# A row of attention scores on all partitions: one transpose for four batches and GpSimd partition broadcasts, in place of four transposes

## The chip, the core and the metric

The kernel runs on one core of a Trainium2 chip. The core has five engines that work side by side and wait for one another by semaphores: PE (TensorE, matrix products and transposes, with its weight loads shown as PEld), DVE (VectorE), ACT (ScalarE), POOL (GpSimd) and SP (SyncE, which only issues DMAs here). The metric is the device time of one launch in microseconds. A profile records one execution; its span runs from the first to the last instruction.

## The reference, cut to what matters

The input is x, 128 batches of 128 nodes with 256 features in float32, and adj, a 128 x 128 matrix of 0 and 1 for every batch. There are four layers, each followed by `x = layernorm(x + layer(x, adj))`. The first is a gated graph network: three steps of a product with the adjacency and a GRU cell. The other three are graph attention layers, which differ only in details; one of them is

```python
def _L1_gnn_ref(h, adj, W, a):
    Wh = jnp.einsum('bnf,of->bno', h, W)
    a1, a2 = (a[:Fout], a[Fout:])
    f_i = Wh @ a1
    f_j = Wh @ a2
    e = f_i[:, :, None] + f_j[:, None, :]
    e = jnp.where(e > 0, e, ALPHA * e)
    e = jnp.where(adj == 0, NEG_INF, e)
    attention = jax.nn.softmax(e, axis=2)
    h_prime = jnp.einsum('bij,bjo->bio', attention, Wh)
```

The change concerns the line that makes e. The nodes i lie on the partitions, so f_i is one number per partition. f_j has to stand as a row, the same on every partition. It is at first computed as one number per partition too.

## The kernel before

**Tiling.** Four batches make a group (G = 4), so a group's tensors are 128 partitions by 512 columns (4 x 128 nodes) or by 1024 (4 x 256 features). There are 32 groups. For each, `gru(g)` describes the three recurrent steps and the first layer norm, and `gat(g)` the three attention layers.

**Order.** The loops do not emit instructions. They describe operations to a planner (`Plan`): the engines that can do it with a duration for each in ns, the buffers read and written, and a priority. `Plan.order()` then runs a list schedule with these durations over all 32 groups at once, takes the most urgent ready operation for each engine, hands out buffers from fixed pools (26 of tag `k2`, 18 of `k4`, 3 PSUM banks of tag `bank`, and so on), and the instructions are emitted in that order. On the chip each engine works through its own list in order. So whatever an operation waits for holds up everything behind it on its engine. Three settings shape the order:

- `LATENCY` adds 200 to 250 ns where an operation follows one on another engine. `MARGIN`, 300 ns, is added on top for operations of PE only.
- `own` reserves buffers of each tag for the oldest stage still at work. There is one setting for recurrent stages and one for attention stages.
- `stage(g, n)` gives the priority. It is g for the first 28 groups, so an older group goes first; the last four groups (`LAST = 4`) go step by step together instead.

Operations of POOL, and those of DVE that are marked `port=BOTH`, are never planned at the same time.

**One attention layer of one group**, by lines. L635 multiplies x by a weight vector and sums along the row, eight times (four batches, f_j first and then f_i), into the small tile f with columns [batch, 0 for f_i and 1 for f_j]. In layers 1 and 2, L639 scales f by the reciprocal deviation of the rows, which POOL makes as a power at L389. L648 makes the rows: for each batch a transpose by PE of the column of f_j, repeated 128 times, into a PSUM bank. L653 adds the mask to it, writes e and takes the row maximum (DVE, one per batch). L657 adds f_i and applies the leaky slope (ACT). L666 and L670 make the negative maximum (DVE, 4 columns). L674 takes the exponential with its sum (ACT). L681 transposes e on PE, L686, L690 or the copy of L287/L289 take it out of PSUM, L711 multiplies it by x, L722 by the layer's weights, and L728 adds the residual. L417 to L428 and L389 then give the next deviation. L473 holds the products of the GRU, L478 the sums over them, L443 the sums of block halves that these products need, L526 the products with the adjacency, L607 and L380 further transposes. The two small additions of L401 (layer norm) and L421 (first attention layer) run on POOL.

Of the kernel before, what the change touches and what calls it, by code (L numbers as in the profile page):

```python
# [1 line left out]

# [20 lines left out]

FAR = -5.0 * 2.0 ** 97
EPS = 1e-5
SLOPE = 0.2
# [21 lines left out]
class Plan:  # L48
# [4 lines left out]

    LATENCY = {"PE": 250, "ACT": 220, "DVE": 200, "POOL": 250, "SP": 4000}

    MARGIN = 300

    def __init__(self, slots, own):
        self.free = {t: list(range(n)) for t, n in slots.items()}
# [139 lines left out]
def adj_resnorm_kernel(  # L199
# [14 lines left out]
    nc = tc.nc  # L214
    B = x.shape[0]
    NG = B // G
    LAST = 4
# [48 lines left out]
    wa = here(consts.tile([P, 3, 2, D], F32, name="wa"))  # L266
# [126 lines left out]
    def layernorm(y, dst, prio):  # L393
        mv, ve, shift = Buf("mv", G, 2), Buf("v", G), Buf("v", G)
        for b in range(G):
            st = Buf("st", 6)
            plan.op({"DVE": 330}, lambda e, b=b, st=st: nc.vector.bn_stats(T(st), T(y)[:, b, :]),
                    reads=[(y, b)], writes=[st], prio=prio)
            plan.op({"DVE": 110}, lambda e, b=b, st=st: nc.vector.bn_aggr(T(mv)[:, b, :], T(st)),
                    reads=[st], writes=[(mv, b)], prio=prio)  # L400
        plan.op({"POOL": 229}, lambda e: nc.gpsimd.tensor_scalar(T(ve), T(mv)[:, :, 1], EPS, None, op0=ALU.add),  # L401
                reads=[(mv, b) for b in range(G)], writes=[ve], prio=prio)
        rstd = power(ve, prio)
        plan.op({"DVE": 100}, lambda e: nc.vector.scalar_tensor_tensor(
            T(shift), T(mv)[:, :, 0], -1.0, T(rstd), op0=ALU.mult, op1=ALU.mult),
            reads=[(mv, b) for b in range(G)] + [rstd], writes=[shift], prio=prio)
        for b in range(G):
            plan.op({"ACT": 500}, lambda e, b=b: nc.scalar.activation(  # L408
                T(dst)[:, b, :], T(y)[:, b, :], AF.Identity, bias=T(shift)[:, b:b + 1], scale=T(rstd)[:, b:b + 1]),
                reads=[(y, b), shift, rstd], writes=[(dst, b)], prio=prio)  # L410

    def deviation(y, before, prio):

        ss, ve = Buf("v", G), Buf("v", G)
        for b in range(G):
            jx = Buf("jx", D)
            plan.op({"ACT": 490}, lambda e, b=b, jx=jx: nc.scalar.activation(  # L417
                T(jx), T(y)[:, b, :], AF.Square, accum_out=T(ss)[:, b:b + 1]),
                reads=[(y, b)], writes=[jx, (ss, b)], prio=prio)
        if before is None:  # L420
            plan.op({"POOL": 229}, lambda e: nc.gpsimd.tensor_scalar(  # L421
                T(ve), T(ss), 1.0 / D, EPS, op0=ALU.mult, op1=ALU.add),
                reads=[(ss, b) for b in range(G)], writes=[ve], prio=prio)
        else:
            eps = Buf("v", G)
            plan.op({"DVE": 100}, lambda e: nc.vector.tensor_scalar(T(eps), T(before), EPS, None, op0=ALU.mult),
                    reads=[before], writes=[eps], prio=prio)
            plan.op({"DVE": 100}, lambda e: nc.vector.scalar_tensor_tensor(  # L428
                T(ve), T(ss), 1.0 / D, T(eps), op0=ALU.mult, op1=ALU.add),
                reads=[(ss, b) for b in range(G)] + [eps], writes=[ve], prio=prio)  # L430
        return ve
# [191 lines left out]
    def gat(g, xc, no, stage):  # L623


        ve, rstd = None, None
        for l in range(3):
            prio = stage(g, STEPS + l)
            if g == 0:
                score_weights(l, prio)  # L630
            f = Buf("f", G, 2)
            for h in (1, 0):
                for b in range(G):
                    fx = Buf("fx", D)
                    plan.op({"DVE": 345}, lambda e, b=b, h=h, l=l, f=f, fx=fx, xc=xc: nc.vector.scalar_tensor_tensor(  # L635
                        T(fx), T(xc)[:, b, :], 1.0, T(wa)[:, l, h, :], op0=ALU.mult, op1=ALU.mult,
                        accum_out=T(f)[:, b, h:h + 1]), reads=[(xc, b), (wa, l)], writes=[fx, (f, 2 * b + h)], prio=prio, port=BOTH)
                if l:
                    plan.op({"DVE": 100}, lambda e, h=h, f=f, rstd=rstd: nc.vector.tensor_mul(  # L639
                        T(f)[:, :, h], T(f)[:, :, h], T(rstd)), reads=[(f, 2 * b + h) for b in range(G)] + [rstd],  # L640
                        writes=[(f, 2 * b + h) for b in range(G)], prio=prio)
# [4 lines left out]
            def fn(e, b_=b_, f=f):  # L646
                for b in range(G):
                    nc.tensor.transpose(T(b_)[:, b * P:(b + 1) * P],  # L648
                                        T(f)[:, b, 1:2].to_broadcast([P, P]), ident)
            plan.op({"PE": 440}, fn, reads=[(f, 2 * b + 1) for b in range(G)], writes=[b_], prio=prio)  # L650

            for b in range(G):
                plan.op({"DVE": 215}, lambda e, b_=b_, b=b, e_=e_, top=top: nc.vector.tensor_tensor_reduce(  # L653
                    T(e_)[:, b, :], T(b_)[:, b * P:(b + 1) * P], T(no)[:, b, :], 1.0, 3 * FAR, ALU.add, ALU.max,
                    T(top)[:, b:b + 1]), reads=[b_, no], writes=[(e_, b), (top, b)], prio=prio)
            for b in range(G):
                plan.op({"ACT": 285}, lambda e, b=b, f=f, e_=e_: nc.scalar.activation(  # L657
                    T(e_)[:, b, :], T(e_)[:, b, :], AF.Prelu, bias=T(f)[:, b, 0:1], alpha=SLOPE),
                    reads=[(f, 2 * b), (e_, b)], writes=[(e_, b)], prio=prio)
            if l == 1:  # L660

# [2 lines left out]
                    T(some), T(top), 0.5 * FAR, None, op0=ALU.is_gt),  # L664
                    reads=[(top, b) for b in range(G)], writes=[some], prio=prio)
            plan.op({"DVE": 100}, lambda e, f=f, top=top: nc.vector.scalar_tensor_tensor(  # L666
                T(top), T(top), -1.0, T(f)[:, :, 0], op0=ALU.mult, op1=ALU.subtract),
                reads=[(top, b) for b in range(G)] + [(f, 2 * b) for b in range(G)],
                writes=[(top, b) for b in range(G)], prio=prio)
            plan.op({"DVE": 100}, lambda e, top=top, nmax=nmax: nc.vector.scalar_tensor_tensor(  # L670
                T(nmax), T(top), SLOPE, T(top), op0=ALU.mult, op1=ALU.min),
                reads=[(top, b) for b in range(G)], writes=[nmax], prio=prio)
            for b in range(G):
                plan.op({"ACT": 390}, lambda e, b=b, e_=e_, nmax=nmax, den=den: nc.scalar.activation(  # L674
                    T(e_)[:, b, :], T(e_)[:, b, :], AF.Exp, bias=T(nmax)[:, b:b + 1],
                    accum_out=T(den)[:, b:b + 1]), reads=[(e_, b), nmax], writes=[(e_, b), (den, b)], prio=prio)
            b_ = bank()
# [74 lines left out]

# [41 lines left out]
```

## Time and profile before

| what | us |
|---|---|
| median of 3 runs (2683.05 to 2686.83) | 2685.42 |
| the profiled execution, whole | 2684.54 |
| its span | 2682.8 |
| mean granted TensorE clock | 0.996 of full speed |
| L648, the four transposes: 384 instructions on PE | 58.2 busy |
| L473, the GRU products on PE | 2400.3 busy, two groups of 4032 |
| L653 on DVE: 384 instructions | 89.2 busy |
| POOL in all: 618 instructions | 549.7 busy |

Busy times of PE are sums of durations of matmuls that overlap, as these are pipelined; starts in a timeline show what one of them holds. A line name such as L648 is a line of the kernel file before. In a row of groups the columns are line, engine, operation, output and inputs, shapes and count, then busy us and mean ns, then the idle time of the engine just before, and what ended it.

### The profile page before, as it was taken

Reading aid. Unit: us, or ns where it says so; the run is one execution under the profiler, and the core shown is the slowest. Engines: PE = TensorE matmul, PEld = TensorE weight load, DVE = VectorE, ACT = ScalarE, POOL = GpSimd, SP = SyncE. Lnnn points to the kernel's source line nnn. Section 1 sums busy time; section 2 is a strip of 40 time slices with the busy share of each in tenths; the row PEclk is TensorE's granted clock in tenths of the full one; section 3 lists DMA queues with packets and bytes.
Section 4 is the critical chain, followed back from the end, with each engine's and each line's share of the span. In section 5 each row is a group of like instructions: output and inputs, shape, how many; then the busy total and the mean of one; then the engine's idle time right before and its main releaser. Section 6 shows DMA issues by size and latency. Waiting matters only on the chain.

```text
span 2682.8 us, 41895 instructions
## 1 busy us (share of the span) xinstructions
PE 2650.4 (99%) x14536; PEld 2367.5 (88%) x14536; DVE 2069.0 (77%) x6111; ACT 1611.6 (60%) x4453; POOL 549.7 (20%) x618
## 2 busy tenths in 40 slices
PE   8999999999999999999999999999999999999988
PEld 7888888898898888898889888988988898988877
DVE  5677677887777877778877778777878777786787
ACT  4555666565656666566556566656666665655467
POOL 1122122221122221122211122211222211231111
PEclk9999999999999999999999999999999999999999
DMA  3100000000000000000000001000000000000000
GB/s 110 32 17 20 28 13 28 21 25 28 14 27 21 24 28 21 21 28 21 24 28 21 21 20 28 24 22 19 29 21 25 28 21 17 19 6 24 17 1 32
DMA packets 70102, 65.35 MB, mean 24 GB/s; under 512 B 2689, under 2 KB 68225, under 8 KB 69889
## 3 DMA queue, kind: packets, MB, share of 16 engines
q1 hardware_dynamic: 69456, 62.66, 7.7%
q8 instruction: 114, 1.87, 0.3%
q14 instruction: 100, 0.81, 0.1%
q10 hardware_dynamic: 432, 0.01, 0.0%
HBM read 45.89 MB, written 16.78 MB: 23 GB/s over the span
## 4 chain that ended last, share of the span: by engine, by line
PE 93%; DVE 4%; ACT 1%; issue 1%; DMA 0%; POOL 0%; POOLq 0%; SPq 0%; ACTq 0%; DVEq 0%
PE gate L473 63%; PE bank L722 11%; PE bank L526 6%; PE bank L711 6%; PE bank L607 3%; PE bank L681 1%; PE bank L648 1%; DVE fx L635 1%; PE bank L380 1%; PE bank L338 1%; DVE k L728 1%; DVE k L289 0%; DVE k L568 0%; DVE k L478 0%; DVE k L653 0%
## 5 line engine op out<-in xcount | busy, mean ns | idle before, releaser
L473 PE MATMUL gate<-k,whs 128*128 128x256 f32 x4032 | 1201.1, 380 | 2.4 <-DVE k L478 1.9
L473 PE MATMUL gate<-k,wcs 128*128 128x256 f32 x4032 | 1199.2, 379 | 0.0
L473 PEld LDWEIGHTS gate<-k,wcs 128*128 128x128 f32 x4032 | 766.1, 190 | 104.0
L473 PEld LDWEIGHTS gate<-k,whs 128*128 128x128 f32 x4032 | 730.4, 190 | 84.5 <-DVE k L478 3.1
L478 DVE TENSOR_TENSOR k<-gate,k 128x512 f32<-128x512 f32 x576 | 389.3, 684 | 207.9 <-PE gate L473 184.0
L287 ACT COPY k<-bank 128x512 f32<-128x512 f32 (+1 forms) x401 | 229.5, 584 | 206.8 <-PE bank L607 91.3
L722 PE MATMUL bank<-gwT,k 128*128 128x256 f32 x1536 | 348.8, 380 | 1.0 <-DVE k L289 0.8
L722 PEld LDWEIGHTS bank<-gwT,k 128*128 128x128 f32 x1536 | 290.4, 190 | 42.2 <-DVE k L289 1.8
L552 ACT ACTIVATE k<-k,brz 128x512 f32<-128x512 f32 (+1 forms) x384 | 225.6, 622 | 166.3 <-DVE k L478 164.7
L389 POOL TENSOR_TENSOR v<-v,neghalf 128x4 f32<-128x4 f32 x128 | 134.4, 1050 | 857.7 <-DVE v L428 840.3
L635 DVE SCALAR_TENSOR_TENSOR fx<-k,wa 128x256 f32<-128x256 f32 x768 | 285.9, 426 | 24.3 <-ACT k L408 24.2
L417 ACT ACTIVATE jx<-k 128x256 f32<-128x256 f32 x384 | 156.5, 408 | 231.0 <-DVE k L728 230.7
L534 ACT COPY k<-gate 128x512 f32<-128x512 f32 x288 | 167.6, 582 | 192.8 <-PE gate L473 188.4
L443 POOL TENSOR_TENSOR k<-k,k 128x256 f32<-128x256 f32 x229 | 175.9, 789 | 450.0 <-DVE k L289 223.2
L728 DVE SCALAR_TENSOR_TENSOR k<-bank,v,k 128x256 f32<-128x256 f32 x384 | 167.2, 476 | 106.8 <-PE bank L722 106.6
L289 DVE COPY k<-bank 128x512 f32<-128x512 f32 x219 | 150.1, 686 | 114.0 <-PE bank L711 88.6
L586 POOL TENSOR_TENSOR k<-k,k 128x512 f32<-128x512 f32 x90 | 133.3, 1492 | 303.4 <-ACT k L581 284.2
L711 PEld LDWEIGHTS bank<-k,k 128*128 128x128 f32 x1536 | 187.6, 194 | 7.7 <-DVE k L728 1.9
L711 PE MATMUL bank<-k,k 128*128 128x128 f32 x1536 | 191.2, 278 | 2.2 <-DVE k L728 1.1
L588 DVE SCALAR_TENSOR_TENSOR k<-k,k 128x512 f32<-128x512 f32 x192 | 170.1, 886 | 2.2 <-POOL k L586 1.1
L674 ACT ACTIVATE k<-k,v 128x128 f32<-128x128 f32 x384 | 148.9, 389 | 30.8 <-DVE v L670 30.2
L581 ACT ACTIVATE k<-k,bi 128x512 f32<-128x512 f32 x192 | 138.3, 721 | 47.1 <-DVE k L578 36.9
(86 smaller groups left out, 3012.9 us busy)
## 6 DMA issues: line engine op xcount, KB each, us to landing
xs<-in_x_dram SPq DMA_DIRECT2D x32, 512.0 KB, 3.8
k<-in_x_dram SPq DMA_DIRECT2D x32, 512.0 KB, 3.8
out_dram<-k SPq DMA_DIRECT2D x32, 512.0 KB, 2.9
adj<-in_adj_dram SPq DMA_DIRECT2D x32, 256.0 KB, 2.8
k<-in_gnn_wT_dram SPq DMA_DIRECT2D x3, 256.0 KB, 4.8
k<-in_w_ihT_dram SPq DMA_DIRECT2D x2, 384.0 KB, 5.8
k<-in_w_hhT_dram SPq DMA_DIRECT2D x2, 384.0 KB, 6.0
k<-in_gat_w_dram SPq DMA_DIRECT2D x3, 256.0 KB, 4.6
```

What stands on the lines that cost most here:

```text
L287: nc.scalar.copy(dst, src)
L443: nc.vector if e == "DVE" else nc.gpsimd).tensor_tensor(T(t)[:, j, :], a(), b(), ALU.subtract),
L473: nc.tensor.matmul(T(dst)[:, j * H:(j + 1) * H], T(w)[:, m, gt, :], moving(m, ms)[1](), start=first and n == 0, stop=n == len(todo) - 1, s ...
L478: plan.op({"DVE": 630}, lambda e: nc.vector.tensor_add(T(o)[:, :, j * H:(j + 1) * H], T(b_).rearrange("p (g n) -> p g n", g=2), T(part).re ...
L526: nc.tensor.matmul(T(b_)[:, b * P:(b + 1) * P], src, T(am)[:, b, :], start=True, stop=True)
L534: plan.op({"ACT": 500}, lambda e: nc.scalar.copy(T(dst), T(src)), reads=[src], writes=[(dst, 0), (dst, 1)], prio=prio)
L552: nc.scalar.activation(T(o)[:, gt, n0:n1], src(), AF.Tanh, bias=brz[:, gt * KC + c:gt * KC + c + 1], scale=0.5)
L588: plan.op({"DVE": 620}, lambda e, d=d, o=o: nc.vector.scalar_tensor_tensor(T(d), T(o)[:, 1, :], 1.0, T(d), op0=ALU.add, op1=ALU.mult), rea ...
L635: plan.op({"DVE": 345}, lambda e, b=b, h=h, l=l, f=f, fx=fx, xc=xc: nc.vector.scalar_tensor_tensor(T(fx), T(xc)[:, b, :], 1.0, T(wa)[:, l, ...
L711: nc.tensor.matmul(T(b_)[:, b * P:(b + 1) * P], T(xc)[:, b, c * P:(c + 1) * P], T(pT)[:, b, :], start=True, stop=True)
L722: nc.tensor.matmul(T(b_)[:, (b - b0) * D:(b - b0 + 1) * D], T(aT[k])[:, b * P:(b + 1) * P], T(gwT)[:, l, k, :], start=(k == 0), stop=(k == ...
L728: nc.vector.scalar_tensor_tensor(T(y)[:, b, :], T(b_)[:, (b - b0) * D:(b - b0 + 1) * D], T(rden)[:, b:b + 1], T(xc)[:, b, :], op0=ALU.mult ...
```

## The change

For the first 28 groups, f is 128 columns wide (32 per batch, zero but for two), f_j is now column 0 of a batch's 32 and f_i column 1. One transpose of the whole f puts the f_j of batch b on partition 32 b. ACT or DVE copies this 128 x 128 block from PSUM to a buffer of tag `k2` (`row`), and four `partition_broadcast` on POOL spread one partition each over the 128 partitions of e, where the operation of L653 then reads it and writes it in place. The last four groups keep the four transposes. POOL's broadcast belongs to a library that is loaded once at the start, after the identity matrix has been made; the two additions [...] move from POOL to DVE. The planner's settings change with it: MARGIN, the reserved buffers, and a priority that is 1.5 groups earlier for attention stages.

```diff
-    MARGIN = 300
+    MARGIN = 500
...
-    own = ({"k2": 12, "k4": 5, "gate": 2, "v": 5, "fx": 0, "jx": 0, "st": 0}, {"k2": 4, "k4": 3, "v": 5, "fx": 0, "jx": 0, "st": 0})
-    floats = {"gru": 0, "k4": 1024, "xs": 1024, "fx": 256, "jx": 256, "f": 8, "mv": 8, "st": 6, "v": 4}
+    own = ({"k2": 9, "k4": 4, "gate": 2, "bank": 1, "v": 5, "fx": 0, "jx": 0, "st": 0}, {"k2": 2, "k4": 2, "bank": 1, "v": 5, "fx": 0, "jx": 0, "st": 0})
+    floats = {"gru": 0, "k4": 1024, "xs": 1024, "fx": 256, "jx": 256, "f": 128, "mv": 8, "st": 6, "v": 4}
...
+    for t in slots["f"]:
+        nc.vector.memset(t, 0.0)
...
     ident = consts.tile([P, P], F32)
-    make_identity(nc, ident)
...
-        plan.op({"POOL": 229}, lambda e: nc.gpsimd.tensor_scalar(T(ve), T(mv)[:, :, 1], EPS, None, op0=ALU.add),
+        plan.op({"DVE": 100}, lambda e: nc.vector.tensor_scalar(T(ve), T(mv)[:, :, 1], EPS, None, op0=ALU.add),
...
-            plan.op({"POOL": 229}, lambda e: nc.gpsimd.tensor_scalar(
+            plan.op({"DVE": 100}, lambda e: nc.vector.tensor_scalar(
...
-            f = Buf("f", G, 2)
+            f = Buf("f", G, P // G)
...
-                        accum_out=T(f)[:, b, h:h + 1]), reads=[(xc, b), (wa, l)], writes=[fx, (f, 2 * b + h)], prio=prio, port=BOTH)
+                        accum_out=T(f)[:, b, 1 - h:2 - h]), reads=[(xc, b), (wa, l)], writes=[fx, (f, 2 * b + h)], prio=prio, port=BOTH)
...
+            if g < NG - LAST:
+
+                plan.op({"PE": 115}, lambda e, b_=b_, f=f: nc.tensor.transpose(
+                    T(b_)[:, 0:P], T(f).rearrange("p b h -> p (b h)"), ident),
+                    reads=[(f, 2 * b + 1) for b in range(G)], writes=[b_], prio=prio)
+                row = Buf("k2", P)
+                plan.op({"ACT": 250, "DVE": 200}, lambda e, b_=b_, row=row: copy(e, T(row), T(b_)[:, 0:P]),
+                        reads=[b_], writes=[row], prio=prio)
                 for b in range(G):
-                    nc.tensor.transpose(T(b_)[:, b * P:(b + 1) * P],
-                                        T(f)[:, b, 1:2].to_broadcast([P, P]), ident)
-            plan.op({"PE": 440}, fn, reads=[(f, 2 * b + 1) for b in range(G)], writes=[b_], prio=prio)
+                    plan.op({"POOL": 300}, lambda e, row=row, b=b, e_=e_: nc.gpsimd.partition_broadcast(
+                        T(e_)[:, b, :], T(row)[b * P // G:b * P // G + 1, 0:P]), reads=[row], writes=[(e_, b)], prio=prio)
+                rows, keys, port = (lambda b, e_=e_: T(e_)[:, b, :]), lambda b: [], BOTH
+            else:
+                def fn(e, b_=b_, f=f):
+                    for b in range(G):
+                        nc.tensor.transpose(T(b_)[:, b * P:(b + 1) * P],
+                                            T(f)[:, b, 0:1].to_broadcast([P, P]), ident)
+                plan.op({"PE": 440}, fn, reads=[(f, 2 * b + 1) for b in range(G)], writes=[b_], prio=prio)
+                rows, keys, port = (lambda b, b_=b_: T(b_)[:, b * P:(b + 1) * P]), lambda b, b_=b_: [b_], ("POOL",)
...
-                plan.op({"DVE": 215}, lambda e, b_=b_, b=b, e_=e_, top=top: nc.vector.tensor_tensor_reduce(
-                    T(e_)[:, b, :], T(b_)[:, b * P:(b + 1) * P], T(no)[:, b, :], 1.0, 3 * FAR, ALU.add, ALU.max,
-                    T(top)[:, b:b + 1]), reads=[b_, no], writes=[(e_, b), (top, b)], prio=prio)
+                plan.op({"DVE": 215}, lambda e, rows=rows, b=b, e_=e_, top=top: nc.vector.tensor_tensor_reduce(
+                    T(e_)[:, b, :], rows(b), T(no)[:, b, :], 1.0, 3 * FAR, ALU.add, ALU.max,
+                    T(top)[:, b:b + 1]), reads=keys(b) + [no, (e_, b)], writes=[(e_, b), (top, b)], prio=prio, port=port)
...
-        return g if g < tail else tail + n, 2 * g + (n >= STEPS)
+        return (g + (-1.5 if n >= STEPS else 0) if g < tail else tail + n), 2 * g + (n >= STEPS)
...
+        make_identity(nc, ident)
+
+        nc.gpsimd.load_library(library_config.all_libraries[10])
```

More of the change, by code (lines that the diff above doesn't have):

```diff
@@ L4 @@
 import concourse.tile as tile
+from concourse import library_config
 from concourse import mybir
@@ L636, in gat @@
                         T(fx), T(xc)[:, b, :], 1.0, T(wa)[:, l, h, :], op0=ALU.mult, op1=ALU.mult,
-                        accum_out=T(f)[:, b, h:h + 1]), reads=[(xc, b), (wa, l)], writes=[fx, (f, 2 * b + h)], prio=prio, port=BOTH)
+                        accum_out=T(f)[:, b, 1 - h:2 - h]), reads=[(xc, b), (wa, l)], writes=[fx, (f, 2 * b + h)], prio=prio, port=BOTH)
                 if l:
                     plan.op({"DVE": 100}, lambda e, h=h, f=f, rstd=rstd: nc.vector.tensor_mul(
-                        T(f)[:, :, h], T(f)[:, :, h], T(rstd)), reads=[(f, 2 * b + h) for b in range(G)] + [rstd],
+                        T(f)[:, :, 1 - h], T(f)[:, :, 1 - h], T(rstd)), reads=[(f, 2 * b + h) for b in range(G)] + [rstd],
                         writes=[(f, 2 * b + h) for b in range(G)], prio=prio)
@@ L644, in gat @@
             b_ = bank()
-            def fn(e, b_=b_, f=f):
-                for b in range(G):
-                    nc.tensor.transpose(T(b_)[:, b * P:(b + 1) * P],
-                                        T(f)[:, b, 1:2].to_broadcast([P, P]), ident)
-            plan.op({"PE": 440}, fn, reads=[(f, 2 * b + 1) for b in range(G)], writes=[b_], prio=prio)
+            if g < NG - LAST:
[5 more added lines that the diff above has]
+                        reads=[b_], writes=[row], prio=prio)
+                for b in range(G):
+                    plan.op({"POOL": 300}, lambda e, row=row, b=b, e_=e_: nc.gpsimd.partition_broadcast(
[8 more added lines that the diff above has]
+                rows, keys, port = (lambda b, b_=b_: T(b_)[:, b * P:(b + 1) * P]), lambda b, b_=b_: [b_], ("POOL",)
@@ L656, in gat @@
             for b in range(G):
                 plan.op({"ACT": 285}, lambda e, b=b, f=f, e_=e_: nc.scalar.activation(
-                    T(e_)[:, b, :], T(e_)[:, b, :], AF.Prelu, bias=T(f)[:, b, 0:1], alpha=SLOPE),
+                    T(e_)[:, b, :], T(e_)[:, b, :], AF.Prelu, bias=T(f)[:, b, 1:2], alpha=SLOPE),
                     reads=[(f, 2 * b), (e_, b)], writes=[(e_, b)], prio=prio)
@@ L666, in gat @@
             plan.op({"DVE": 100}, lambda e, f=f, top=top: nc.vector.scalar_tensor_tensor(
-                T(top), T(top), -1.0, T(f)[:, :, 0], op0=ALU.mult, op1=ALU.subtract),
+                T(top), T(top), -1.0, T(f)[:, :, 1], op0=ALU.mult, op1=ALU.subtract),
                 reads=[(top, b) for b in range(G)] + [(f, 2 * b) for b in range(G)],
```

## The prediction, made before the changed kernel was run

> **What bounds the kernel now.** I read the page first: busy times, the slices, the chain that ended last.
>
> ```profile
> span 2682.8 us, 41895 instructions
> PE 2650.4 (99%) x14536; PEld 2367.5 (88%) x14536; DVE 2069.0 (77%) x6111; ACT 1611.6 (60%) x4453; POOL 549.7 (20%) x618
> PE 93%; DVE 4%; ACT 1%; issue 1%; DMA 0%; POOL 0%; POOLq 0%; SPq 0%; ACTq 0%; DVEq 0%
> ```
>
> PE is busy all the time and carries 93% of the chain. A busy PE need not be a useful one, so next come the busy times by stretches of 81.6 us, which is one group's period (in the timeline the same work returns every 81.6 us). Columns after the stretch: its length, then busy us of PE, PEld, DVE, ACT, POOL.
>
> ```profile
> 0.00:81.60 81.60, 73.56 (x347) 60.87 (x348) 45.40 (x94) 37.55 (x76) 12.83 (x20) 0.98 0.32 104
> 408.00:489.60 81.60, 79.64 (x430) 70.48 (x429) 61.89 (x182) 48.45 (x134) 16.23 (x18) 1.00 0.07 23
> 1143.00:1224.60 81.60, 81.60 (x453) 73.36 (x452) 64.19 (x190) 49.80 (x140) 16.88 (x19) 1.00 0.08 24
> 2526.40:2608.00 81.60, 74.44 (x381) 63.71 (x380) 70.40 (x248) 50.77 (x143) 14.44 (x18) 0.95 0.01 2
> 2608.00:2682.80 74.80, 63.49 (x377) 54.97 (x375) 58.24 (x300) 54.66 (x215) 10.76 (x12) 0.96 0.09 29
> ```
>
> In the steady part PE has no gap, while DVE (79%), ACT (61%) and POOL (21%) wait for it. PE's 32 idle us lie at the two ends: 14 in the first six periods, 18 in the last two. So in the middle every us taken from PE is a us of the result, as long as its inputs come in time. The PE timeline shows what a set of four transposes holds:
>
> ```profile
> 1018.07 0.59 PE L473 MATMUL gate<-k,wcs 128*128 128x256 f32 x2
> 1018.50 0.60 PE L648 MATMUL bank<-ident,f 128*128 128x128 f32 x4
> 1018.94 0.60 PE L473 MATMUL gate<-k,whs 128*128 128x256 f32 x2
> 1024.12 0.60 PE L681 MATMUL bank<-ident,k 128*128 128x128 f32 x4
> ```
>
> From 1018.50 to 1018.94 are 0.44 us for four; where two such sets follow one another (starts 1003.69, 1004.13, 1004.56) they take 0.87. I take 0.108 us each. The 274 ns of the group's row below overlap, since matmuls are pipelined, and are not a price.
>
> [...]
>
> **The change part by part.** The rows that I price from:
>
> ```profile
> L648 PE MATMUL bank<-ident,f 128*128 128x128 f32 x384 | 58.2, 274 | 1.6 <-DVE f L639 1.3 <-DVE k L728 0.2
> L653 DVE CUSTOM_DVE_ANT_0 k<-bank,am 128x128 f32<-128x128 f32 x384 | 89.2, 287 | 62.2 <-PE bank L648 62.1
> L690 ACT ACTIVATE k<-bank,v 128x128 f32<-128x128 f32 x132 | 37.6, 367 | 59.3 <-PE bank L681 59.2
> L389 POOL TENSOR_TENSOR v<-v,neghalf 128x4 f32<-128x4 f32 x128 | 134.4, 1050 | 857.7 <-DVE v L428 840.3
> ```
>
> Removed: groups 0 to 27, three layers each, are 84 places; three of four transposes go at each, 252 x 0.108 = 27.2 us of PE. The last four groups keep theirs. Per period that is nine, 0.97 us, so 81.6 becomes 80.6.
>
> Added on other engines: 84 row copies (ACT 0.37 by L690, DVE some 0.29 by L653's columns; 45 on ACT, 39 on DVE in the new order), 336 broadcasts on POOL, 64 four-column operations moved from POOL (250 and 360 ns) to DVE (some 165 ns). Per period that is DVE +0.8 us on 64.2, ACT +0.6 on 49.8, POOL +5 on 16.9: no engine nears 80.6. Their cover is PE itself.
>
> Latency is what counts. In the steady part before, DVE's first L653 begins 0.20 us after PE has left the transposes, and the last exponential ends at 1022.42:
>
> ```profile
> 1019.14 0.29 DVE L653 CUSTOM_DVE_ANT_0 k<-bank,am 128x128 f32<-128x128 f32 x1 [1.39 <-PE bank L648]
> 1022.23 0.19 ACT L674 ACTIVATION_READ_ACCUMULATOR k<-k,v 128x1 f32 x1
> ```
>
> That is 3.5 us after PE left L648, and PE took up L681 at 1024.12, 5.2 after: 1.7 spare. After: 0.20, copy 0.37, hand-over 0.1, four broadcasts 4b, four L653 at 0.21 (start to start), 2.44 for the rest to the exponentials' end: 3.95 + 4b, in the worst case that no L653 overlaps a broadcast. With b = 0.45: 5.75 us. I counted the changed kernel's PE instructions between each of the 84 new transposes and the L681 set that follows, at the spacings of before (0.108 a transpose, 0.222 a 128-column matmul, 0.432 a pair of L473 or L722): 7.8 us of cover in the median, 6.9 at the lower quartile, 6.1 at the twentieth, 4.8 at the least; before it was 5.2 in the median. So the order gives 2.6 us more cover and the chain needs 2.3. Only the place with 4.8 falls short, by 0.95. What stands behind a DVE instruction that waits for POOL (in the new order often a copy out of PSUM or an L478 sum that frees a gate bank) is what PE waits for next; MARGIN, up from 300 to 500 ns, is its cover in the plan.
>
> Unknown: b, from 0.3 (the plan's own figure) to 1.05 (L389); I take 0.45. Loading the library: POOL's first sums begin at 6.89 and must be done when PE's first L473 starts at 19.41; they end at 12.73, so 6.7 us lie free. [...] Moving make_identity changes nothing in POOL's order; the memsets of f run before the first inputs land at 5 us, the wider f and the exchange of its two columns add no instruction: nothing. L653 now reads SBUF twice instead of PSUM and SBUF: [...] twelve in a period, on an engine with 16 us free: nothing on the path. The other quotas, the priority g - 1.5 and MARGIN change the order of PE everywhere: the strictly periodic order of before is gone. The one irregular stretch of before outside start and tail, 163 to 490, loses 2.4 us of 326. At that rate the 2150 us of the middle would lose 16; with a better margin and earlier attention work it could be 0. I take 4. At the tail, two of the twelve attention layers of the last groups now come between products of the recurrent stage: worth 0 to -4, I take -1.
>
> Sum against the profiled execution: 2682.8 - 27.2 + 4 - 1 = 2658.6 of span. The profiled run took 1.7 more (2684.54), the median of the three runs 2.6 more (2685.42). Forecast 2661 us.
>
> **Rivals.**
> (a) The broadcast is slow and becomes the wait: slower. Place: between the new transpose and L681, in PE's own queue. Over the 84 covers counted above, a chain of 7.55 us falls short by 0.32 us on average, and 84 x 0.32 eats the 27 us: it decides from b = 0.90. At L389's 1.05 the chain is 8.15 and the mean shortfall 0.68, so 57 us are given back: 2661 - 1 + 57, about 2717. For: POOL's four-column power takes 1.05, and its operations wait for DVE. Against: a power is arithmetic, and a copy of 128 columns should stay below L443's 0.79.
> (b) The irregular order gives back more: 16 us at the stretch's rate instead of 4, so 2661 + 12, about 2673. For: in 163 to 490 PE waits for DVE's L653, L478, L639. Against: MARGIN.
> (c) DVE falls behind: [...] Even 12 x 0.5 us leaves DVE at 71 of 80.6, so it hurts only as jitter: a quarter us of PE at each of the 84 places is 21 us, about 2681, next to no change. For: 39 copies of the row stand on DVE with L653 right behind them, so DVE sits out the broadcasts. Against: the cover above.
> (d) The middle gives nothing back and the ends improve by 6 us more: 2682.8 - 27.2 - 6 + 2.6, about 2652. For: of the 14 us at the start only the 8 that PE waits for x are out of reach. Against: the order of the tail hardly differs.
>
> **How the numbers follow.** Forecast, 2655 to 2668: 0.62. (d): 0.08. (b) and the milder half of (c): 0.13. No change, within 0.2% (2680.0 to 2690.8), about what runs of this kernel can tell apart: 0.05. (a), slower: 0.12. Faster is then 0.83. The range leaves out (a) and the far end of (d): 2651 to 2683.
>
> **What would show it.** Right: 84 single transposes and 12 sets of four remain, PE's busy time falls by some 27 us, the middle shows full PE windows at 80.6 us per group, and the broadcasts start less than 0.6 us apart [...]. Wrong: PE waits at L681's successor for ACT, or at matmuls for DVE copies queued behind a wait for POOL; broadcasts spaced 1 us; a long gap in POOL near the start that moves PE's first products past 19.4.

## The result, and the profile after

| | before | after |
|---|---|---|
| median of ten runs each, us | 2685.35 (2682.95 to 2687.07) | 2677.72 (2675.72 to 2680.05) |
| profiled execution, whole / its span | 2684.54 / 2682.8 | 2675.88 / 2673.7 |
| PE busy / PE idle in the span | 2650.4 / 32.4 | 2628.0 / 45.7 |

The ratio is 0.9973, with a 95% interval of 0.9963 to 0.9982: 7.6 us faster, where 24 were forecast. First the page of the changed kernel: span, busy times, and the chain that ended last.

```profile
span 2673.7 us, 42034 instructions
PE 2628.0 (98%) x14284; PEld 2338.9 (87%) x14284; DVE 2093.9 (78%) x6172; ACT 1639.7 (61%) x4554; POOL 647.1 (24%) x901
PE 88%; DVE 9%; issue 1%; ACT 1%; POOL 0%; POOLq 0%; ACTq 0%; DVEq 0%
```

252 matmuls are gone, as the change says, and PE's busy time fell by 22.4 us. But PE idles for 13.3 us more, and DVE's share of the chain has gone from 4% to 9%. No engine has taken PE's place: DVE is as far from full as before (78% busy, 77% before). The busy times by stretches say where the idle time lies (columns: stretch, length, then busy us of PE, PEld, DVE, ACT, POOL, the granted clock, the DMA share, GB/s).

```profile
0.00:81.60 81.60, 71.66 (x340) 59.56 (x341) 42.30 (x93) 37.58 (x77) 10.81 (x17) 1.00 0.33 104
816.00:897.60 81.60, 77.00 (x429) 68.48 (x428) 63.85 (x179) 45.35 (x122) 22.34 (x31) 1.00 0.12 36
1143.00:1224.60 81.60, 81.59 (x446) 72.96 (x445) 67.52 (x210) 51.34 (x143) 21.22 (x33) 1.00 0.10 30
2526.40:2608.00 81.60, 74.17 (x393) 63.85 (x392) 70.87 (x284) 55.81 (x163) 11.30 (x11) 0.98 0.00 1
```

Before, each stretch of the middle was full. Now some are (1143) and some miss 4.6 us (816), and no stretch looks like the next. The waits of PE in the changed kernel name what it waited for (columns: us in all, times, the longest).

```profile
PE bank L383 <- POOL ident masks.py:199: 9.9, 1, 9.9
PE bank L650 <- DVE fx L638: 5.9, 8, 2.2
PE gate L476 <- DVE k L481: 2.6, 3, 1.1
PE bank L610 <- DVE k L594: 2.4, 3, 1.1
PE bank L650 <- DVE f L642: 2.0, 1, 2.0
...
PE bank L610 <- DVE v L679: 1.7, 1, 1.7
```

(In the changed kernel L650 is the single transpose, L657 the broadcast, L669 the score operation that was L653, L663 the four transposes of the last groups; L638 and L642 compute f, were L635 and L639; L476, L481, L594, L610, L446 were L473, L478, L591, L607, L443; L292 and L383 were L289 and L380.) The first line is at the start, and comes up with the library below. The other lines shown are waits for DVE (those for ACT, which are left out here, come to 3.5 us in all). The largest part, 7.9 us, stands at L650, ahead of the broadcasts: there PE waits for f, not for what the broadcasts deliver.

To put a size on each part I counted, from all starts on PE, how much longer an instruction held PE than its usual spacing (0.215 us for 256 columns, twice that for 512, 0.11 for 128 and for a transpose). Excess of more than 0.05 us counts as lost, and so does the time before PE's first instruction. This catches also the part of a wait that the profile does not show as idle time.

| us lost on PE | start, to 163 | middle, 163 to 2450 | tail |
|---|---|---|---|
| before | 15.2 | 5.3 | 21.0 |
| after | 12.9 | 29.1 | 17.6 |

So 27.2 us of transposes went, 23.8 came back in the middle, and start and tail gave 2.3 and 3.4: minus 9.1 in all, which is what the spans differ by.

### The profile page after: what moved, and what is told of

The parts are those of the page before. It is cut to its first block, busy times and chain, and to the rows that moved or that the text cites. A ratio compares the mean times of both kernels' runs of the same rounds, so it can differ in the third digit from the quotient of the medians.

```text
span 2673.7 us, 42034 instructions
## 1 busy us (share of the span) xinstructions
PE 2628.0 (98%) x14284; PEld 2338.9 (87%) x14284; DVE 2093.9 (78%) x6172; ACT 1639.7 (61%) x4554; POOL 647.1 (24%) x901
## 4 chain that ended last, share of the span: by engine, by line
PE 88%; DVE 9%; issue 1%; ACT 1%; POOL 0%; POOLq 0%; ACTq 0%; DVEq 0%
PE gate L476 61%; PE bank L738 11%; PE bank L727 5%; PE bank L529 5%; PE bank L610 3%; DVE fx L638 2%; PE bank L697 1%; DVE k L481 1%; DVE k L669 1%; DVE k L744 1%; PE bank L383 1%; DVE k L292 1%; DVE k L571 1%; DVE k L594 0%; DVE k L591 0%
## 5 line engine op out<-in xcount | busy, mean ns | idle before, releaser
L476 PE MATMUL gate<-k,whs 128*128 128x256 f32 x4032 | 1201.8, 380 | 3.2 <-DVE k L481 2.6
L476 PE MATMUL gate<-k,wcs 128*128 128x256 f32 x4032 | 1199.2, 379 | 0.0
L476 PEld LDWEIGHTS gate<-k,wcs 128*128 128x128 f32 x4032 | 766.1, 190 | 104.0
L476 PEld LDWEIGHTS gate<-k,whs 128*128 128x128 f32 x4032 | 730.6, 190 | 91.1 <-DVE k L481 4.5
L481 DVE TENSOR_TENSOR k<-gate,k 128x512 f32<-128x512 f32 x576 | 391.3, 685 | 240.7 <-PE gate L476 204.3
L290 ACT COPY k<-bank 128x512 f32<-128x512 f32 (+1 forms) x473 | 255.5, 551 | 230.4 <-PE bank L529 68.8
L638 DVE SCALAR_TENSOR_TENSOR fx<-k,wa 128x256 f32<-128x256 f32 x768 | 297.9, 436 | 11.4 <-ACT k L411 9.2
L446 POOL TENSOR_TENSOR k<-k,k 128x256 f32<-128x256 f32 x245 | 206.4, 858 | 250.6 <-DVE k L594 70.5
L537 ACT COPY k<-gate 128x512 f32<-128x512 f32 x288 | 166.4, 581 | 161.8 <-PE gate L476 160.4
L292 DVE COPY k<-bank 128x512 f32<-128x512 f32 (+1 forms) x231 | 141.0, 616 | 59.7 <-PE bank L650 20.5
L589 POOL TENSOR_TENSOR k<-k,k 128x512 f32<-128x512 f32 x74 | 98.2, 1329 | 358.8 <-ACT k L584 300.7
L657 POOL PARTITION_BROADCAST k<-k x336 | 115.3, 443 | 216.1 <-ACT k L290 125.4
```

The source lines that it names most:

```text
L446: nc.vector if e == "DVE" else nc.gpsimd).tensor_tensor(T(t)[:, j, :], a(), b(), ALU.subtract),
L476: nc.tensor.matmul(T(dst)[:, j * H:(j + 1) * H], T(w)[:, m, gt, :], moving(m, ms)[1](), start=first and n == 0, stop=n == len(todo) - 1, s ...
L481: plan.op({"DVE": 630}, lambda e: nc.vector.tensor_add(T(o)[:, :, j * H:(j + 1) * H], T(b_).rearrange("p (g n) -> p g n", g=2), T(part).re ...
L537: plan.op({"ACT": 500}, lambda e: nc.scalar.copy(T(dst), T(src)), reads=[src], writes=[(dst, 0), (dst, 1)], prio=prio)
```

## The experiments

All times are medians, with the kernel before run on the same chip in the same sitting: 2683.41 us for the first four, 2683.59 for the next four, 2685.03 for the last four. The changed kernel ran in the sitting of the result (2677.72) and in the last one (2678.61). Distances to it are taken from 2677.72 and cross sittings, between which the kernel before moved by up to 1.9 us. Three explanations were open: the saving is smaller than counted; the broadcasts and the waits for them give it back; the new order gives it back, whatever is in it. Later the library joined them.

**One transpose in the order of before.** Where the changed kernel has one transpose, this one has batch 0's alone, in the old order, and the score operations of all four batches read its row.

```diff
-                for b in range(G):
+                for b in range(1 if g < NG - LAST else G):
...
-                    T(e_)[:, b, :], T(b_)[:, b * P:(b + 1) * P], T(no)[:, b, :], ...
+                    T(e_)[:, b, :], T(b_)[:, (0 if g < NG - LAST else b) * P:(1 if g < NG - LAST else b + 1) * P], T(no)[:, b, :], ...
```

> The kernel before with its order untouched; in the first 28 groups only the transpose of batch 0 is issued and the rows of the other three batches are left out (all four score operations read batch 0's row). Theory A (the order costs the gain): the saving is real where the order is kept, 252 x 0.108 = 27 us, so 2656 to 2660 us, PE's middle without gaps. Theory B (the broadcasts cost it): the same 2656 to 2660, since there are none. Rival C (the removed transposes were worth less than 0.108 us each on PE): above 2668.

2659.44 us (2658.59 to 2660.02), ratio 0.9909 [0.9894, 0.9924]. Its busy times in a long stretch of the middle and in one period:

```profile
489.60:2284.80 1795.20, 1795.20 (x9866) 1612.33 (x9865) 1432.73 (x4238) 1099.29 (x3071) 381.48 (x429) 1.00 0.08 24
816.00:897.60 81.60, 81.60 (x449) 73.27 (x449) 65.14 (x193) 50.40 (x141) 16.87 (x19) 1.00 0.07 23
```

PE has no gap and the time falls by 24.0 us. From one set of transposes to the same set of the next group, the starts at L648 lie 80.62 us apart, where they lay 81.61 apart before: nine transposes at 0.11 us. The transposes are worth what was counted, if the order lets PE keep it.

**The new settings around the old operations.** The changed planner's numbers, with four transposes in all groups, no broadcast and no library.

```diff
-            if g < NG - LAST:
+            if g < 0:
...
-        nc.gpsimd.load_library(library_config.all_libraries[10])
```

> The changed kernel with the old four transposes in every group, no row copy, no broadcast and no library, but with the new MARGIN, reserved buffers, priority and the two additions on DVE. Theory A: the order is what loses, and it loses here too, so slower than before by 10 to 25 us: 2695 to 2710. Theory B: the same as before, 2683 to 2689.

2719.41 us (2715.87 to 2722.13), ratio 1.0132 [1.0119, 1.0146]: 36 us slower than before, with nothing computed differently, and slower than either expectation. The same long stretch, first of the kernel before, then of this one:

```profile
489.60:2284.80 1795.20, 1795.20 (x9945) 1613.80 (x9944) 1412.03 (x4180) 1095.42 (x3037) 371.57 (x418) 1.00 0.08 23
489.60:2284.80 1795.20, 1778.10 (x9793) 1592.16 (x9792) 1389.84 (x4102) 1098.40 (x3042) 384.64 (x404) 1.00 0.08 23
```

17 us of gaps have come into a stretch that had none, with POOL as idle as before. By the count of the starts the middle loses 43.6 us, 38.3 more than before. An order alone can therefore cost more than the transposes are worth; what the numbers do to another set of operations need not be the same, so the next two kernels keep the changed kernel's operations.

**The broadcasts left out, the order kept.** POOL gets nothing at their places, and the score operation reads the mask twice.

```diff
-                    plan.op({"POOL": 300}, lambda e, row=row, b=b, e_=e_: nc.gpsimd.partition_broadcast(
-                        T(e_)[:, b, :], T(row)[b * P // G:b * P // G + 1, 0:P]), reads=[row], writes=[(e_, b)], prio=prio)
-                rows, keys, port = (lambda b, e_=e_: T(e_)[:, b, :]), lambda b: [], BOTH
+                    plan.op({"POOL": 300}, lambda e: None, reads=[row], writes=[(e_, b)], prio=prio)
+                rows, keys, port = (lambda b: T(no)[:, b, :]), lambda b: [], BOTH
```

> The changed kernel in its own order, but the 336 broadcasts are not issued and the score operation reads the mask twice instead of the row. Theory A: PE's gaps stay where they are, 2672 to 2678 us. Theory B: [...] 10 us or more are won: 2667 or less.

2673.06 us (2671.55 to 2673.33), ratio 0.9959 [0.9947, 0.9972]: 4.7 us below the changed kernel (3.8 us if the two ratios are compared). Waits of PE in this kernel:

```profile
PE bank L650 <- DVE fx L638: 5.9, 8, 2.2
PE bank L650 <- DVE f L642: 2.5, 1, 2.5
PE bank L610 <- DVE k L594: 2.5, 3, 1.1
```

The same eight waits of 5.9 us stand there with no broadcast in the program. With the broadcasts go all waits for them, and some 4 to 5 us; the rest of the loss is not theirs.

**The same operations in a settled order.** The planner's numbers were searched until its order of PE repeated (it does so every two groups here, in 162.02 us); the operations are those of the changed kernel.

```diff
-    MARGIN = 500
+    MARGIN = 700
...
-    own = ({"k2": 9, "k4": 4, "gate": 2, "bank": 1, ...}, {"k2": 2, "k4": 2, "bank": 1, ...})
+    own = ({"k2": 9, "k4": 3, "gate": 2, "bank": 1, ...}, {"k2": 0, "k4": 1, "bank": 1, ...})
...
-                    plan.op({"POOL": 300}, lambda e, row=row, b=b, e_=e_: nc.gpsimd.partition_broadcast(
+                    plan.op({"POOL": 330}, lambda e, row=row, b=b, e_=e_: nc.gpsimd.partition_broadcast(
...
-        return (g + (-1.5 if n >= STEPS else 0) if g < tail else tail + n), 2 * g + (n >= STEPS)
+        return (g + (0 if n >= STEPS else 0) if g < tail else tail + n), 2 * g + (n >= STEPS)
```

> The changed kernel with all its broadcasts; only planner numbers differ (MARGIN 700, no earlier priority for attention, other reserved buffers, 330 ns for a broadcast), chosen so that the order of PE repeats in every group. Theory A: the middle has no gaps and the whole saving stays: 2652 to 2660 us, a period of 80.6 us. Theory B: the broadcasts cost here what they cost in the changed kernel: 2672 to 2680.

2662.91 us (2662.52 to 2663.32), ratio 0.9923 [0.991, 0.9935]: 14.8 us below the changed kernel, and 2.9 above the range expected. Its long stretch, beside that of the changed kernel:

```profile
489.60:2284.80 1795.20, 1791.74 (x9825) 1603.92 (x9825) 1414.61 (x4180) 1100.87 (x3038) 529.83 (x740) 1.00 0.08 24
```

```profile
489.60:2284.80 1795.20, 1780.45 (x9743) 1590.50 (x9742) 1432.95 (x4206) 1115.89 (x3111) 472.03 (x667) 1.00 0.08 24
```

PE's gaps shrink from 14.8 to 3.5 us although POOL works more, and what is left comes back in step:

```profile
PE bank L650 <- DVE f L642: 3.5, 11, 0.3
```

Eleven waits of 0.3 us, one in every two groups. That is not all: a group takes 81.0 us here, not the 80.6 that were expected and that the kernel with one transpose in the order of before has. So this order too gives back 0.4 us in each group, most of it in longer spacings of starts rather than in idle time. Busy us of PE in eleven successive stretches of 163.2 us, from 489.6 on, show what "settled" means:

| kernel | | | | | | | | | | | |
|---|---|---|---|---|---|---|---|---|---|---|---|
| before | 163.2 | 163.2 | 163.2 | 163.2 | 163.2 | 163.2 | 163.2 | 163.2 | 163.2 | 163.2 | 163.2 |
| after | 161.8 | 163.2 | 158.6 | 162.5 | 162.3 | 161.9 | 162.2 | 163.2 | 162.5 | 161.2 | 161.2 |
| new settings, old operations | 158.5 | 162.0 | 161.7 | 160.1 | 162.8 | 160.3 | 162.6 | 163.2 | 162.6 | 163.2 | 161.0 |
| settled | 162.9 | 162.9 | 162.9 | 162.9 | 162.9 | 162.9 | 162.9 | 162.9 | 162.9 | 162.9 | 162.9 |

The sequence of PE's instructions between 480 and 2290 us says it more sharply. Before, every instruction is of the same line as the one a group earlier. In the settled order 99.6% are of the same line as the one two groups earlier. In the changed kernel no shift near one or two groups gives more than 37%, and 40% with the new settings around the old operations.

**The broadcasts under the old settings.** The changed operations with MARGIN, quotas and priority of before.

```diff
-    MARGIN = 500
+    MARGIN = 300
...
-    own = ({"k2": 9, "k4": 4, "gate": 2, "bank": 1, ...}, {"k2": 2, "k4": 2, "bank": 1, ...})
+    own = ({"k2": 12, "k4": 5, "gate": 2, ...}, {"k2": 4, "k4": 3, ...})
...
-        return (g + (-1.5 if n >= STEPS else 0) if g < tail else tail + n), 2 * g + (n >= STEPS)
+        return (g + (0 if n >= STEPS else 0) if g < tail else tail + n), 2 * g + (n >= STEPS)
```

> The changed kernel with its transposes, copies and broadcasts, but MARGIN 300, the old reserved buffers and no earlier priority. Theory A (each set of numbers gives another order, and the order decides): no settled order is found with these numbers either, gaps of 30 us in the middle, 2685 to 2700 us, slower than the changed kernel. Theory D (the new numbers, not the new operations, spoil the order): the order of before comes back and the time falls to 2658 to 2668.

2700.81 us (2698.71 to 2702.83), ratio 1.0063 [1.0049, 1.0077], and 22.7 us of gaps in the long stretch:

```profile
489.60:2284.80 1795.20, 1772.53 (x9628) 1580.94 (x9627) 1425.64 (x4174) 1105.76 (x3071) 477.99 (x666) 1.00 0.08 23
```

PE's sequence does not repeat here either (44% at best, near one or two groups). Neither set of numbers fits both sets of operations: the old numbers lose with the new operations, the new ones with the old. So the changed kernel's numbers do help its operations, by 23 us, and the order that they give is still far from the best.

**The start.** In the changed kernel's timeline (start, length, engine, what, and in brackets the idle time before it and what ended it) the identity matrix is late:

```profile
0.72 0.20 POOL masks.py:197 MEMSET ident<- 128x128 f32 x1 [0.29 <-POOLq L802]
9.56 0.28 POOL masks.py:199 TENSOR_SCALAR_AFFINE_SELECT ident<-ident 128x128 f32<-128x128 f32 x1 [8.63 <-issue]
9.89 1.97 PE L383 MATMUL bank<-ident,xs 128*128 128x128 f32 x8 [9.89 <-POOL ident masks.py:199]
15.25 0.71 POOL L446 TENSOR_TENSOR k<-k 128x256 f32<-128x256 f32 x1 [5.41 <-issue]
20.68 0.59 PE L476 MATMUL gate<-k,whs 128*128 128x256 f32 x2
```

Two gaps end in POOL's own "issue": 8.63 us ahead of the affine select and 5.41 us ahead of the first sum. Before, neither was there, and PE's first transpose began with the arrival of x:

```profile
1.00 0.29 POOL masks.py:199 TENSOR_SCALAR_AFFINE_SELECT ident<-ident 128x128 f32<-128x128 f32 x1
5.10 1.94 PE L380 MATMUL bank<-ident,xs 128*128 128x128 f32 x8 [5.10 <-DMA xs<-in_x_dram]
```

With the new settings around the old operations, a kernel that loads no library, the affine select begins at 1.01 too. The second gap stands where the program loads the broadcast's library, between the identity and POOL's first sum. What POOL does in the first is not shown: no run records a load itself or the state that a launch finds. That both come with the library is an inference from kernels that lack them. The one above loads no library; two of the next load it first and build the identity behind it by an iota on POOL and a comparison on DVE, one in the settled order, one in the changed kernel's:

```diff
-        make_identity(nc, ident)
-
         nc.gpsimd.load_library(library_config.all_libraries[10])
+        nc.gpsimd.iota(ident, pattern=[[-1, P]], base=0, channel_multiplier=1, allow_small_or_imprecise_dtypes=True)
+        nc.vector.tensor_scalar(ident, ident, 0.0, None, op0=ALU.is_equal)
```

> e4 with the identity made by iota on GpSimd and a comparison on DVE[...]. Theory S1 (the late start is mostly hidden by the loads of the weights): PE's first transpose at 5 us instead of 10, but the time falls by 0 to 2 us: 2661 to 2663. Theory S2 (the late start goes through to the end): 4 to 5 us less, 2657 to 2659.

> The changed kernel with the identity of e6. S1: 2675 to 2678 us. S2: 2672 to 2673.

In the settled order: 2659.2 us (2658.87 to 2659.57), ratio 0.9908 [0.9893, 0.9923], 3.7 us less than with the old identity. The intervals of the two ratios overlap a little, but no run of one kernel comes near those of the other, also in the repeat below. In the changed kernel: 2674.51 us (2673.63 to 2675.51), ratio 0.9966 [0.9953, 0.9978], 3.2 us less and between the two expectations; the intervals overlap widely, so it counts only as agreeing. The start of the settled kernel with this identity:

```profile
0.86 0.24 POOL L767 IOTA ident<- 128x128 f32 x1 [0.43 <-POOLq L802]
6.17 1.97 PE L383 MATMUL bank<-ident,xs 128*128 128x128 f32 x8 [6.17 <-DVE ident L768]
7.99 0.73 POOL L446 TENSOR_TENSOR k<-k 128x256 f32<-128x256 f32 x1 [6.89 <-ACT k L290]
17.89 0.59 PE L476 MATMUL gate<-k,whs 128*128 128x256 f32 x2
```

Both issue gaps are gone, the iota runs at 0.86, and the first product comes at 17.89, where the settled order had 21.01 with the old identity.

The last of the four puts the library into the kernel before, ahead of the planner's first operation, and moves the two small additions to DVE:

```diff
+        nc.gpsimd.load_library(library_config.all_libraries[10])
...
-        plan.op({"POOL": 229}, lambda e: nc.gpsimd.tensor_scalar(T(ve), T(mv)[:, :, 1], EPS, None, op0=ALU.add),
+        plan.op({"POOL": 229}, lambda e: nc.vector.tensor_scalar(T(ve), T(mv)[:, :, 1], EPS, None, op0=ALU.add),
...
-            plan.op({"POOL": 229}, lambda e: nc.gpsimd.tensor_scalar(
+            plan.op({"POOL": 229}, lambda e: nc.vector.tensor_scalar(
```

> The kernel before, with the library of the broadcasts loaded at the start after the identity and the two four-column additions emitted on DVE; no broadcasts. PE's first transpose moves from 5.1 to about 10 us[...]. S1: 2684 to 2687 us; S2: 2688 to 2690.

2693.99 us (2692.88 to 2696.11), ratio 1.0039 [1.0026, 1.0052]: 10.4 us slower than before, more than either expectation. Its affine select:

```profile
16.80 0.28 POOL masks.py:199 TENSOR_SCALAR_AFFINE_SELECT ident<-ident 128x128 f32<-128x128 f32 x1 [15.88 <-issue]
```

15.88 us are 1.8 more than the two gaps of the changed kernel (14.04), and no such gap follows behind the affine select. So all of it falls ahead of the identity here, although the text of the program makes the identity first; why, is not shown. The middle is untouched, since PE is busy in all 1795.20 us of the long stretch, and by the count of the starts 8.8 us of the loss lie at the start. The size was missed, not the sign: what the library costs here is paid at the start, where PE waits for the identity.

**The last four runs.** The settled order with the new identity was taken as a base. One kernel has five last groups with the old transposes in place of four, one leaves the broadcasts out as above, two repeat.

```diff
-    LAST = 4
+    LAST = 5
```

> e6 with LAST = 5, so the last five groups instead of four go step by step (and keep the four transposes, 9 more on PE, 1 us). PE's idle time in the last 130 us was some 22 us in e6. Theory T (the tail's order leaves more than it must): 2 to 4 us less than e6, 2655 to 2657. Rival: DVE carries the tail whatever the order, 2659 to 2661.

> e6 in its own order with the 336 broadcasts not issued and the mask read twice. In the changed kernel leaving them out won 4.7 us. Theory A: in an order with slack at these places they cost nothing, 2657 to 2660 us, as e6. Theory B': [...] 2654 to 2656.

> The changed kernel as it is, on the same chip as the others of this call: 2675 to 2679 us; the gap to e6 (2659) and to e7 (2674.5) is then read without a change of session.

> e6 as it is, for comparison within this call: 2658 to 2660 us.

Without broadcasts: 2659.00 us (2658.47 to 2659.26), ratio 0.9904 [0.9889, 0.9919]; with them, again, 2658.78 us (2658.39 to 2659.05), ratio 0.9904 [0.989, 0.9917]. In a settled order the broadcasts cost nothing that can be measured; in the changed kernel's they cost 4 to 5 us. The changed kernel again: 2678.61 us (2676.42 to 2680.3), ratio 0.9976 [0.9966, 0.9986].

Five last groups: 2656.92 us (2655.97 to 2657.05), ratio 0.9896 [0.9883, 0.991], the fastest of all kernels here, 1.9 us below the one with four and 28.1 below before. The stretch of the tail, first with four last groups, then with five, both in the settled order with the new identity:

```profile
2529.60:2611.20 81.60, 71.02 (x391) 61.58 (x390) 77.78 (x358) 56.63 (x199) 12.69 (x11) 0.94 0.00 1
```

```profile
2529.60:2611.20 81.60, 74.37 (x431) 65.38 (x430) 77.62 (x408) 63.20 (x230) 11.27 (x10) 0.96 0.01 1
```

DVE is at 95% of this stretch in both, and PE goes from 87% to 91%: the tail is the one place where DVE is near to being the bound. Not all of the 28 us is the worth of the transposes, since the settings of before were not searched in the same way.

## Why the prediction was right or wrong

**Where the sum went wrong.** The forecast of the span was 2658.6 us, and 2673.7 were measured, 15.1 more. By the count of the starts the middle gave back 23.8 us in place of 4 (19.8 more), the tail brought 3.4 in place of 1, and the start brought 2.3 that the sum did not have. So one term, the order, makes the error.

**Saving, 27.2 us: right.** 252 matmuls went, and with the order of before they bring 24.0 us in the median and 24.6 in the span; there middle and tail lose 2.7 us more than before by the count of the starts.

**The broadcast, b = 0.45 us: too high, on the safe side.** The value was my estimate, between the plan's 0.3 and the 1.05 of L389; nothing in the trace of before shows a broadcast. In the changed kernel a set of four takes 1.34 us in the median of 84 sets, and one starts 0.29 after another; the row's 443 ns overlap, so they are not the spacing. Rival (a), the slow broadcast, fell.

**The cover of the chain: right.** PE never waited more than 0.6 us at L697, where the exponentials arrive.

**The irregular order, "I take 4", bounds 0 and 16: this step failed.** The middle gives back 23.8 us, six times the value taken and more than the upper bound. I had measured the loss rate in the one irregular stretch of before (2.4 us in 326), counted only idle time there, and then let MARGIN argue it down. The experiments showed that the order is the term that decides: the same operations took 2662.9, 2677.7 and 2700.8 us under three sets of planner's numbers, and the changed kernel's numbers around the old operations cost 36. One place of the changed kernel shows how (timeline of DVE, POOL and PE):

```profile
820.84 0.93 DVE L638 SCALAR_TENSOR_TENSOR fx<-k,wa 128x256 f32<-128x256 f32 x1
...
821.71 0.68 DVE L591 SCALAR_TENSOR_TENSOR k<-k,k 128x512 f32<-128x512 f32 x1
821.93 0.30 PE L650 MATMUL bank<-ident,f 128*128 128x128 f32 x1 [0.47 <-DVE fx L638]
...
822.75 1.34 POOL L657 PARTITION_BROADCAST k<-k  x4 [1.26 <-DVE k L292]
...
823.21 0.29 DVE L669 CUSTOM_DVE_ANT_0 k<-k,am 128x128 f32<-128x128 f32 x1 [0.55 <-POOL k L657]
...
824.18 0.82 POOL L446 TENSOR_TENSOR k<-k,k 128x256 f32<-128x256 f32 x1
...
824.35 1.21 DVE L594 SCALAR_TENSOR_TENSOR k<-k,k 128x512 f32<-128x512 f32 x1
...
825.70 0.63 PE L610 MATMUL bank<-ident,k 128*128 128x128 f32 x4 [1.71 <-DVE v L679]
```

DVE comes late with f, so PE idles 0.47 us at L650. Then L669 stands 0.55 us for the broadcast, and L594, queued behind the four L669, takes 1.21 us in place of 0.68 while POOL runs a sum (L446 at 824.18). L610 transposes what L594 writes, and PE stands idle for 1.71 us. (The trace names L679, DVE's next instruction, as the one that ended the wait; by the program it is L594.) With the broadcasts left out, this wait is 0.78 us at the same place:

```profile
823.76 0.63 PE L610 MATMUL bank<-ident,k 128*128 128x128 f32 x4 [0.78 <-DVE v L678]
```

This is a wait of the kind that the prediction named as a sign of being wrong: for a DVE operation queued behind a wait for POOL. At this place about half of it came with the broadcasts and half is the order's. DVE had its work too late at a moment when the next instruction in PE's list needed it; that DVE is 22% idle on average doesn't help.

**Rivals (b) and (c).** Their times, 2673 and 2681, lie on either side of the result, and (b)'s mechanism is the right one at one and a half times its size (24 against 16). (c) put the loss behind the broadcasts at each of the 84 places; those are worth 4 to 5 us in the changed kernel, a fifth of the loss. Rival (d) supposed better ends and an untouched middle: the ends did improve, by 5.7 us where it had 6, but the middle did not hold.

**The tail, -1: the direction right, -3.4 measured.**

**The library, for which the sum has no term: a wrong step too.** I placed one load on POOL ahead of its sums and let the 6.7 us that lay free there hide it; how long a load takes was not shown by the trace of before. There are two gaps, 14 us together, and the first lies ahead of the identity, which PE's first transpose needs, not only ahead of the sums. The first product moved from 19.41 to 20.68; in the settled order the two gaps are worth 3.7 us. PE had waited 8.0 us for x at L380 before; in the changed kernel it waits 9.9 us for the identity and 0.5 us for x, so most of the new wait only takes the place of an old one. No further cost came at the first broadcast: the first four took 1.36 us at 142.29, and 1.34 is the median of all sets.

**The score operation with two SBUF inputs, nothing on the path: nearly right.** No wait of PE is put down to L669, but it has 1% of the chain, where L653 had less than half a per cent. 287 ns became 352 in the mean:

```profile
L669 DVE CUSTOM_DVE_ANT_0 k<-k,am 128x128 f32<-128x128 f32 x336 | 107.9, 352 | 16.1 <-POOL k L657 15.2
```

The two SBUF inputs by themselves add nothing: with POOL idle it takes 285 ns in the middle (102 cases), and the form that reads PSUM took 288 in the kernel before (172 cases). Beside POOL's sums it takes 625 ns in the mean (44 cases), and the form that reads PSUM took 288 (66 cases).

**What stays open.** Which of MARGIN, quotas, priority and the planned price of a broadcast unsettles the order was not tried one by one. Two orders whose sequence repeats (that of before and the settled one) lose little, and three that do not repeat lose much; that the repeating itself makes them good, and not the arrival of inputs in time that comes with it, is not shown. Nor is it shown how the 4 to 5 us of the broadcasts divide between DVE's waits for them and the POOL sums that they delay into other DVE operations, or whether the order of before could itself be improved.

## What to carry to other kernels

When one engine is full and follows a list that was written ahead, an operation saved on it is worth its time only if the list still meets its inputs (here the same 252 transposes brought 24.0 us in the order of before and 7.6 with the changed kernel's list and broadcasts): search the planner's numbers again for the new operations, and look at whether its stretches repeat, not only at the mean of busy time. Test the two apart: the old list with the operation left out shows the worth, and the new list with the old operations shows the order's share. Where a kernel loads a GpSimd library at the start, look for POOL's gaps there, see what stands behind them and waits for it (here the identity, behind 8.63 us), and try that one built differently (here 3.7 us less in the settled order).

## What the runs showed of the hardware that was not expected

- With the library in the program POOL has gaps at the start, and the first broadcasts take no longer than others (1.36 us for the first four, 1.34 in the median of all sets). The gaps are, in the five kernels that start like the changed one 8.63 to 10.12 us ahead of the affine select and 5.02 to 5.45 us ahead of the first sum, and 15.88 us in one gap with the library in the kernel before. With the identity from an iota behind the load, in the settled order, POOL idles 0.43 us ahead of the iota and neither gap is there. (In three of the five the trace puts the end of the second gap down to ACT's copy, so the wait for it may be a part.)
- These operations of DVE are stretched beside POOL's sums (L669 from 0.28 to 0.63 us in the mean), and not beside its broadcasts (0.30). From 492 to 2280 us of the changed kernel I sorted four lines of DVE by what POOL did: nothing, or a sum or a broadcast during more than half of the instruction.

| mean us (count) | POOL idle | L446 or L589 on POOL | broadcast on POOL |
|---|---|---|---|
| L638 | 0.42 (449) | 0.69 (44) | 0.42 (1) |
| L591 | 0.68 (100) | 0.99 (24) | 0.68 (1) |
| L594 | 0.68 (112) | 1.04 (12) | 0.68 (2) |
| L669 | 0.28 (102) | 0.63 (44) | 0.30 (103) |

  Some 60% of those beside a sum (76 of 124) took over 1.4 times the shortest of their line, the rest did not; with POOL idle none did, and none of the 107 beside a broadcast. What stretches them beside a sum, and not beside a broadcast, is not shown.
- The idle time of PE shows only a part of a wait. In the middle the idle time is 17.5 us in the changed kernel and 2.8 before, while the loss by starts is 29.1 and 5.3: 23.8 more lost for 14.7 more idle. A matmul is recorded as busy for longer than it holds PE (380 ns in the mean for 256 columns, where starts follow one another every 0.215 us), so the first part of each wait, 0.17 us in the mean of the changed kernel's waits, counts as busy.
